# Row gathers of AUGRU steps 4 to 7 moved into the end of the GRU, one PSUM pool per AUGRU bank, and the first AUGRU stages on named banks

## The chip, the cores and the metric

One of the cores of a Trainium2 chip runs the whole program. The metric is the device time of one execution in microseconds (us). The kernel before takes 2083.58 us, the median of 3 runs (2083.48 to 2083.83).

## The reference

A recommender in the manner of DIEN, for 1024 users with histories of 100 items, 128 features each, all in float32:

```python
# keys: a GRU over the history, T = 100 steps, H = 128
r, z = sigmoid(i_r + h_r), sigmoid(i_z + h_z)
n = tanh(i_n + r * h_n)
h = (1 - z) * n + z * h
# attention: a 512 -> 80 -> 40 -> 1 MLP on [keys, q, keys - q, q * keys], masked softmax over t
pooled = einsum('bt,btd->bd', attn, keys)
att_seq = pooled.T[:T]            # step t's weights are feature t of pooled
# AUGRU over the keys, with step t's weight a_t for each user
r, u = sigmoid([h, x_t] @ Wr.T + br), sigmoid([h, x_t] @ Wu.T + bu)
h_hat = tanh([h * r, x_t] @ Wh.T + bh)
u = a_t * u
h = (1 - u) * h + u * h_hat
# the state at each user's last item goes with user, item and history sums into a
# 640 -> 200 -> 80 -> 1 MLP of sigmoids
```

The weights of the AUGRU's first step are a feature of the finished pooled sum. So the AUGRU's recurrence cannot begin before the softmax over all 100 steps is done.

## The kernel before, in words

**Layout.** Features lie on the 128 partitions, users along the free dimension, in two halves of 512 columns (`HB`, `NH` = 2). A half is one matmul's width and one PSUM bank. Weights and states are float32, for which a matmul appears as two passes in the trace. The order of instructions on each engine is the order in which the program text issues them (`manual_schedule`); pools of tiles say which memory is reused when, and waits follow from that.

**GRU phase** (`gru_phase`). 100 steps, each for both halves: gate matmuls (L490), activations on ACT (L502 to L522), sums on DVE. Around a step lie the attention MLP of earlier steps, the history sums on POOL (L476, L477) and the pooling. Each step's state is transposed in blocks of 32 (`Half.transpose`, L529) into a buffer of four steps, `kt`, pool `kp`, and stored in DRAM as `keys_d`: the first two groups of four steps (q = 0 and 1, which are steps 0 to 3 and 4 to 7) as rows of 512 floats per user, later ones in blocks. The softmax runs over blocks of steps that end at `ENDS`; `Half.pool` multiplies a buffered key by its weight `e` (L586) and adds it to `pooled` (L587), on POOL, and in the tail of the phase (after the loop) on POOL for half 0 and DVE for half 1. The last lines multiply by the lengths' mask into `s_b` (L919) and prepare the stores to `pooled_d`; half 1's four are issued on SP (L923).

**Sorting.** The AUGRU works on users sorted by length, so that late steps are narrower. Rows of `keys_d` and of `pooled_d` come in sorted order by indirect DMAs on POOL (`gather`, L135): 128 rows of 512 floats (256 KB) for a key row gather `rows`, four for each half and q (`load_rows`, L146). The rows of q = 0 are gathered two a step from step 70 (`GATHER`) on; those of q = 1 by `all_of(gathers(1))` in the AUGRU phase.

**AUGRU phase** (`augru_phase`, L925). It begins with the hand-over, in this order of text: `load_key(0, i)` transposes step 0's keys on TensorE (L1006, tile `pk`) and copies them on ACT (L1007); half 0's four stores to `pooled_d` on ACT's queue (L1167); eight gathers of `att_r` from `pooled_d` on POOL; `first_step` (L947, L949), matmuls and activations of step 0, which has no state yet; step 1's keys; `open_gates` (L1020), the input parts of step 1's gates; `first_state` (L962 to L974), which spreads step 0's weights over the partitions by matmuls (`first`, `spare`) and makes the first state h; then the eight row gathers of q = 1. The loop calls `half_step` (L1036) for each step and half: the state's part of the gates (L1024), the reset product, the next half's `open_gates`, loads of the weights of step t + 2, and `load_key(t + 1, i)`. In step 1 `store_weights` also turns `att_r` over (tile `pw` or `spare`, L984), copies it (`att_t`, L986) and stores it for the later loads.

Seven PSUM banks come from one pool `ps3` in turn, an eighth from `pa3`. The GRU phase's tail had six banks from its pool `ps` (`last`) and two from `pa`. SBUF buffers of the AUGRU's keys come from `qp3` (four buffers).

Of the kernel before, what the change touches and what calls it, by code (L numbers as in the profile page):

```python
# [9 lines left out]
F32 = mybir.dt.float32  # L10
# [15 lines left out]
GH = HB // P  # L26

R = 32
KH = HB // R
NK = B // R  # L30
A0, A1 = 80, 40
M0, M1 = 200, 80
# [19 lines left out]
G = 4  # L52
# [3 lines left out]
FIRST = [sum(READ[:q]) for q in range(len(READ))]  # L56
# [9 lines left out]
ALIVE = [[min(HB, 2 * -(-r // (2 * EIGHTH))) for r in room] for room in ROOM] + [[HB] * T]  # L66
WIDTHS = [[max(LEAST, n) for n in alive] for alive in ALIVE]

PR = P // NH


@with_exitstack
def kernel(ctx: ExitStack, tc: tile.TileContext, a: dict, out: bass.AP):
# [26 lines left out]
    nc = tc.nc  # L100
# [21 lines left out]
    ident = const.tile([P, P], F32, name="ident")  # L122
# [5 lines left out]
    idx_p = const.tile([P, HB // PR], I32, name="idx_p")  # L128
    h3 = [const.tile([P, HB], F32, name=f"h3_{i}") for i in range(NH)]
    mid = ctx.enter_context(tc.tile_pool(name="mid", bufs=2))  # L130
    later = {}

    def gather(dst, src, g, i):
# [8 lines left out]
    rows = {}  # L142

    def load_rows(q, i, width, tiles):

        n = READ[q]  # L146
        if q < WHOLE:
            tag = "whole" if q else "once"
            r = rows[q, i] = tiles.tile([P, GH, n * P], F32, tag=tag, name="rows", bufs=NH)
            for g in range(GH):  # L150
                gather(r[:, g, :], keys_d[q], g, i)
                yield
            return
# [12 lines left out]

    def all_of(steps):
        for _ in steps:
            pass

    def gru_phase(pools):
# [31 lines left out]
        hp = pools.enter_context(tc.tile_pool(name="hp", bufs=6))  # L203
        wp = pools.enter_context(tc.tile_pool(name="wp", bufs=2))
        sp = pools.enter_context(tc.tile_pool(name="sp", bufs=2))
        kp = pools.enter_context(tc.tile_pool(name="kp", bufs=8))
        ps = pools.enter_context(tc.tile_pool(name="ps", bufs=6, space=PSUM))
        pa = pools.enter_context(tc.tile_pool(name="pa", bufs=2, space=PSUM))

# [233 lines left out]
        class Half:  # L443
# [85 lines left out]
            def transpose(self, t):  # L529


                q, n = divmod(t, G)
                h = self.h.pop(t) if t < T - 1 else self.h[t]
                if n == 0:
                    self.kt[q] = kp.tile([P, KH, G, R], F32, name="kt")
                kt = self.kt[q]
                nc.vector.transpose(kt[:, :, n, :], h.rearrange("p (k r) -> p k r", r=R))
                if q < WHOLE:
                    to = keys_d[q][self.cols, :].rearrange(
                        "(k r) (n a c) -> n a r k c", r=R, n=G, c=R  # L540
                    )
# [97 lines left out]
        banks = {}  # L639
# [153 lines left out]

        rest = load_later()
        early = [load_rows(0, i, HB, mid) for i in range(NH)]

        late, again, early_from = 6, 24, 84
        for s in range(T):
            last = s == T - 1
            n, due = divmod(s - again, 4)  # L800
            n, i = divmod(n, NH)
# [46 lines left out]
            for half in halves:  # L848
                if last:
                    half.cross_features()  # L850
            for half in halves:
                half.pool(2 if len(half.todo) > 7 or s >= 92 else 1, nc.gpsimd)
                if s >= GATHER:
                    next(early[half.i], None)
# [9 lines left out]
        def some(*these):  # L864
            for f in these:
                next(features[f])

        take(T - 2)
        for half in halves:
            half.product(T - 1)  # L870
# [12 lines left out]
        n = ENDS[-3] - ENDS[-4] + 1  # L883
# [33 lines left out]
        for half in reversed(halves):  # L917
            t = blocked(s_bs[NH * (soft["j"] % 2) + half.i])
            nc.vector.tensor_mul(t, later["used"][:, half.ks, :], pooled[:, half.ks, :])  # L919
            to = pooled_d[half.cols, :].rearrange("(k r) (p c) -> p r k c", r=R, c=R)  # L920
            later["att", half.i] = [(to[p], t[p * R : (p + 1) * R]) for p in range(P // R)]
        for to, t in later["att", 1]:
            nc.sync.dma_start(out=to, in_=t)  # L923

    def augru_phase(pools, widths, alive):  # L925


        wp = pools.enter_context(tc.tile_pool(name="wp3", bufs=3))
        qp = pools.enter_context(tc.tile_pool(name="qp3", bufs=4))
        sp = pools.enter_context(tc.tile_pool(name="sp3", bufs=2))  # L930
        kp = pools.enter_context(tc.tile_pool(name="kp3", bufs=4))
        ps = pools.enter_context(tc.tile_pool(name="ps3", bufs=7, space=PSUM))
        pa = pools.enter_context(tc.tile_pool(name="pa3", bufs=1, space=PSUM))
        wr, wu, wh = later["wr"], later["wu"], later["wh"]
        keys, att, opened, resets, states = {}, {}, {}, {}, {}
        later["pace"] = None

        def bank(name):
            return ps.tile([P, HB], F32, tag="g", name=name)

        def first_step(i):

            k = keys.pop((0, i))
            gates = []
            for n, f in (("u", AF.Sigmoid), ("h", AF.Tanh)):
                p = bank(f"p{n}")
                nc.tensor.matmul(p, lhsT=later["w" + n][:, 1, :], rhs=k, start=True, stop=True)  # L947
# [47 lines left out]
            )  # L995
            att[t, i] = at

        def load_key(t, i):

            q = max(j for j, first in enumerate(FIRST) if first <= t)  # L1000
            w, n, r = widths[t], t - FIRST[q], rows[q, i]
            k = qp.tile([P, HB], F32, name="k3")
            if q < WHOLE:
                p = pa.tile([P, HB], F32, tag="a", name="pk3")
                for g in range(-(-w // P)):
                    nc.tensor.transpose(p[:, ts(g, P)], r[:, g, ts(n, P)], ident)  # L1006
                nc.scalar.copy(k[:, :w], p[:, :w])  # L1007
            else:
                w = -(-w // R)
                nc.vector.transpose(  # L1010
                    k.rearrange("p (k r) -> p k r", r=R)[:, :w, :], r[:, :w, ts(n, R)]
                )
            keys[t, i] = k

        def open_gates(t, i):

            k = keys.pop((t, i))[:, : widths[t]]
            for m, name in ((wr, "pr"), (wh, "ph"), (wu, "pu")):
                p = opened[t, i, name] = bank(name)[:, : widths[t]]
# [15 lines left out]
        def half_step(t, i):  # L1035


            w, h = widths[t], h3[i][:, : widths[t]]
# [30 lines left out]
                store_weights(1, spare)  # L1069
            if t + 2 < T:  # L1070
                load_att(t + 2, i)
            if t + 1 < T:
                load_key(t + 1, i)

        def last_state(i):
# [4 lines left out]
        def predict(g, last=False):  # L1080
# [1 line left out]

            m0, m1 = later["m0"], later["m1"]
            n = M0 // MC
            pool, tag = (ps, "g") if last else (pa, "a")

            def rows_of(out_ap, in_ap, o, i):
                nc.gpsimd.indirect_dma_start(  # L1088
# [10 lines left out]
            p0 = [pool.tile([P, HB], F32, tag=tag, name="p0") for _ in range(n if last else 1)]  # L1099
# [34 lines left out]
            p1 = pool.tile([P, HB], F32, tag=tag, name="p1")[:M1, :P]  # L1134
# [8 lines left out]
            p2 = pool.tile([P, HB], F32, tag=tag, name="p2")[:, 0:1]  # L1143
# [18 lines left out]


        for i in range(NH):
            load_key(0, i)
        for to, t in later["att", 0]:
            nc.scalar.dma_start(out=to, in_=t)  # L1167
# [12 lines left out]
        for t in range(1, T):  # L1180
# [109 lines left out]
```

## Time and profile before

| | |
|---|---|
| median of 3 runs | 2083.58 us |
| profiled execution | 2087.38 us, of which its span 2085.5 us |
| mean granted TensorE clock | 0.993 |
| DVE, ACT, POOL busy | 84%, 40%, 63% of the span |
| DMA | 205.09 MB, mean 98 GB/s |
| a GRU step in mid-phase | 14.07 us |

The profile is one execution. Its page gives each engine's busy time as a share of the span, and the span in 40 slices with a digit for the busy tenths. Groups of instructions by line follow, with the mean time of one and the idle time before it. A timeline lists single instructions: start, length, engine, line, operation, output and inputs, and in brackets the idle time of the engine before it and what ended that. A name such as `ACTq` or `SPq` is the stretch in which an engine issues DMAs; "PEld" is the weight load that goes with a matmul; "remote" and "issue" are idle time that the profile puts down to no instruction of another engine. Ends of matmuls are modelled from their issue.

Some costly groups near the change:

| line, engine | what | number | mean |
|---|---|---|---|
| L586 POOL | key times weight | 191 | 1148 ns |
| L587 POOL | add to pooled | 191 | 1332 ns |
| L490 PE | gate matmul, input part | 1200 | 603 ns |
| L135 POOL | indirect gather, `rows` at 1465 us | 8 | 950 ns, with 300 ns between two |

### The profile page before, as it was taken

What the parts mean: (1) busy time and instruction counts of PE and PEld (TensorE: products, weight loads), DVE (VectorE), ACT (ScalarE), POOL (GpSimd) and SP (SyncE); (2) the same over time, 40 slices, a digit from 0 to 9 for tenths busy, and PEclk for the clock granted to TensorE, in tenths of its full rate; (3) what the DMA queues carried; (4) which work ended last, traced back from release to release, by engine and by line L of the source; (5) the groups of instructions that cost most, each with busy time, mean ns of one, the idle gap of its engine ahead of it and who ended that gap; (6) DMA issues with size and microseconds to landing.
All of it is one profiled execution on the core that took longest, in us unless ns stands there. A gap on an engine that the chain in (4) does not pass through costs nothing. (4 is left out here: it accounts for less than half of the span.)

```text
span 2085.5 us, 26811 instructions
## 1 busy us (share of the span) xinstructions
PE 2039.8 (98%) x8320; PEld 980.6 (47%) x8320; DVE 1755.5 (84%) x3050; ACT 831.7 (40%) x1516; POOL 1304.6 (63%) x1306
## 2 busy tenths in 40 slices
PE   8999999999999999999999999997899999999997
PEld 3343333333333333333333333333444556678897
DVE  6888999989989888989889899997467777888786
ACT  3334343333434333433333343333343444445454
POOL 0234939579796959595969687986635444444332
PEclk9999999999999999999999999998999999999999
DMA  4633233332234334333433222332533333334331
GB/s 119 114 93 100 90 102 110 95 98 84 89 106 112 109 103 121 110 95 110 132 98 102 82 81 89 102 93 72 150 95 110 97 93 96 98 98 97 78 73 35
DMA packets 254324, 205.09 MB, mean 98 GB/s; under 512 B 75814, under 2 KB 216842, under 8 KB 254170
## 3 DMA queue, kind: packets, MB, share of 16 engines
q1 hardware_dynamic: 239738, 170.57, 29.2%
q0 software_dynamic: 12320, 32.44, 5.6%
q8 instruction: 68, 1.11, 0.2%
q14 instruction: 86, 0.70, 0.1%
q10 hardware_dynamic: 2112, 0.26, 0.1%
HBM read 147.16 MB, written 54.40 MB: 97 GB/s over the span
## 5 line engine op out<-in xcount | busy, mean ns | idle before, releaser
L490 PE MATMUL ps<-x,wih 128*128 128x512 f32 x1200 | 592.6, 603 | 4.0 <-DMA x<-in_hist_x 4.0
L490 PE MATMUL ps<-hn,whh 128*128 128x512 f32 x1188 | 574.4, 592 | 0.0
L490 PEld LDWEIGHTS ps<-x,wih 128*128 128x128 f32 x1200 | 220.9, 191 | 327.5 <-issue 253.0
L490 PEld LDWEIGHTS ps<-hn,whh 128*128 128x128 f32 x1188 | 225.7, 190 | 284.1 <-issue 275.8
L476 POOL TENSOR_TENSOR xm<-x,m 128x512 f32<-128x512 f32 x200 | 247.2, 1236 | 136.3 <-DMA m<-mask_d 136.0
L521 ACT ACTIVATE ps<-ps,bih 128x512 f32<-128x512 f32 x200 | 132.4, 662 | 486.6 <-DVE ps L520 486.6
L502 ACT ACTIVATE r<-ps,brz 128x512 f32<-128x512 f32 x200 | 137.5, 687 | 372.9 <-PE ps L490 372.1
L477 POOL TENSOR_TENSOR hist<-hist,xm 128x512 f32<-128x512 f32 x200 | 266.7, 1333 | 15.7
L587 POOL TENSOR_TENSOR pooled<-pooled,kw 128x512 f32<-128x512 f32 x191 | 254.4, 1332 | 15.0
L586 POOL TENSOR_TENSOR kw<-kt,e 128x512 f32<-128x512 f32 x191 | 219.3, 1148 | 70.3 <-DVE e L759 70.2
L159 POOL DMA_INDIRECT rows<-keys_d,idx_k x208 | 202.3, 973 | 83.8 <-POOL rows L158 53.0
L563 DVE TENSOR_TENSOR kq<-hn,item 128x512 f32<-128x512 f32 x200 | 228.5, 1182 | 0.0
L650 PE MATMUL pm<-hn,wk 128*32 128x512 f32 x1200 | 212.0, 596 | 3.5 <-ACT q L233 1.8
L650 PE MATMUL pm<-kq,wkq 128*32 128x512 f32 x1200 | 209.6, 592 | 0.0
L1032 ACT ACTIVATE c<-ph,bh 128x96 f32<-128x96 f32 (+42 forms) x198 | 96.9, 489 | 262.2 <-PE ph L1024 227.7
L650 PE MATMUL pm<-mv,w 128*32 128x512 f32 (+1 forms) x808 | 196.5, 598 | 1.4 <-DVE e L740 1.4
L158 POOL COPY rows<-rest 128x1 f32<-128x1 f32 x208 | 39.1, 188 | 222.1 <-DVE rest L1061 218.1
L1048 DVE TENSOR_TENSOR pu<-pu,c 128x96 f32<-128x96 f32 (+42 forms) x197 | 88.8, 451 | 103.6 <-ACT c L1032 85.0
L684 DVE TENSOR_TENSOR f<-pm,q 128x512 f32<-128x512 f32 x200 | 128.3, 683 | 51.2 <-PE pm L650 51.1
L525 DVE TENSOR_TENSOR d<-hn,ps 128x512 f32<-128x512 f32 x198 | 135.9, 687 | 34.8 <-ACT ps L521 32.5
L526 DVE TENSOR_TENSOR d<-ps,d 128x512 f32<-128x512 f32 x200 | 138.4, 692 | 23.6 <-ACT ps L522 6.4
L520 DVE TENSOR_TENSOR ps<-ps,u 128x512 f32<-128x512 f32 x200 | 140.0, 700 | 21.6 <-PE ps L490 0.5
(180 smaller groups left out, 3028.3 us busy)
## 6 DMA issues: line engine op xcount, KB each, us to landing
x<-in_hist_x SPq DMA_DIRECT2D x212, 256.0 KB
keys_d<-kt SPq DMA_DIRECT2D x46, 1024.0 KB
m<-mask_d SPq DMA_DIRECT2D x200, 128.0 KB
keys_d<-kt SPq DMA_DIRECT2D x64, 64.0 KB
rows<-keys_d,idx_k POOLq DMA_INDIRECT x208
s_b<-mv SPq DMA_DIRECT2D x200, 8.0 KB
mask_i<-in_mask SPq DMA_DIRECT2D x8, 200.0 KB
at<-att_d SPq DMA_DIRECT2D x32, 48.0 KB
```

The source lines that it names most:

```text
L159: nc.gpsimd.indirect_dma_start(out=r[:, k, :], out_offset=None, in_=keys_d[q], in_offset=bass.IndirectOffsetOnAxis(ap=idx_k[:, k, i : i + ...
L476: nc.gpsimd.tensor_mul(d, x, m)
L477: nc.gpsimd.tensor_add(acc, acc, d)
L490: nc.tensor.matmul(p, lhsT=w[:, g, :], rhs=v, start=(j == 0), stop=(j == len(parts) - 1),)
L502: nc.scalar.activation(r, pr, AF.Sigmoid, bias=brz[:, 0:1])
L520: nc.vector.tensor_add(pi, pi, u)
L525: nc.vector.tensor_sub(d, h, pi)
L526: nc.vector.tensor_mul(d, pz, d)
L563: nc.vector.tensor_mul(kq, h, item[:, self.cols])
L586: eng.tensor_mul(d, k, w)
L587: eng.tensor_add(acc, acc, d)
L650: nc.tensor.matmul(p[i][s, :], lhsT=w[:, s], rhs=v, start=start, stop=stop)
```

## The change

The rows of q = 1 are gathered in the GRU phase: four gathers (half 0) in step 98 (`T - 2`) ahead of that step's pooling, four (half 1) after the loop. Their buffers are two `kt` buffers in a pool of its own, `kx`, which also serves the key groups with q % 4 == 1; `kp` shrinks from eight buffers to six. Each AUGRU bank becomes a pool with one buffer; a ring hands them out, and the first stages name their banks. `first_step` and step 1's key copies now stand ahead of half 0's pooled stores on ACT, of which one goes to SP. `open_gates(1, 1)` stands ahead of `open_gates(1, 0)`. Step 2's keys are transposed before `first_state` and no longer in step 1. The pool of AUGRU keys grows from four to six buffers. `predict` takes its banks by a helper, with the same tiles as before.

```diff
+EARLY_BANKS, LATE_BANKS = (2, 5, 6, 0), (3, 4, 1)
...
+    kx = ctx.enter_context(tc.tile_pool(name="kx", bufs=NH))
...
-            tag = "whole" if q else "once"
-            r = rows[q, i] = tiles.tile([P, GH, n * P], F32, tag=tag, name="rows", bufs=NH)
+            tag = "kt" if q else "once"
+            r = rows[q, i] = tiles.tile([P, GH, n * P], F32, tag=tag, name="rows")
...
-        kp = pools.enter_context(tc.tile_pool(name="kp", bufs=8))
+        kp = pools.enter_context(tc.tile_pool(name="kp", bufs=3 * NH))
...
-                    self.kt[q] = kp.tile([P, KH, G, R], F32, name="kt")
+                    self.kt[q] = (kx if q % 4 == 1 else kp).tile(
+                        [P, KH, G, R], F32, tag="kt", name="kt"
+                    )
...
         early = [load_rows(0, i, HB, mid) for i in range(NH)]
+        more_early = [load_rows(1, i, HB, kx) for i in range(NH)]
...
+            if s == T - 2:
+                all_of(more_early[0])
             for half in halves:
                 half.pool(2 if len(half.todo) > 7 or s >= 92 else 1, nc.gpsimd)
...
+        all_of(more_early[1])
         take(T - 2)
...
-        for to, t in later["att", 1]:
+        for to, t in later["att", 1] + later["att", 0][G - 1 :]:
             nc.sync.dma_start(out=to, in_=t)
...
-        qp = pools.enter_context(tc.tile_pool(name="qp3", bufs=4))
+        qp = pools.enter_context(tc.tile_pool(name="qp3", bufs=3 * NH))
...
-        ps = pools.enter_context(tc.tile_pool(name="ps3", bufs=7, space=PSUM))
+        ps = [
+            pools.enter_context(tc.tile_pool(name=f"ps3_{n}", bufs=1, space=PSUM))
+            for n in range(7)
+        ]
...
-        def bank(name):
-            return ps.tile([P, HB], F32, tag="g", name=name)
+        ring = [*LATE_BANKS, *EARLY_BANKS]
+
+        def bank(name, n=None):
+
+            if n is None:
+                n = ring.pop(0)
+                ring.append(n)
+            return ps[n].tile([P, HB], F32, tag="g", name=name)
...
-                p = bank(f"p{n}")
+                p = bank(f"p{n}", EARLY_BANKS[NH * i + j])
...
-                p = pa.tile([P, HB], F32, tag="a", name="pk3")
+                p = pa.tile([P, HB], F32, tag="a", name="pk3") if n is None else bank("pk3", n)
...
-            if t + 1 < T:
+            if 1 < t < T - 1:
                 load_key(t + 1, i)
...
         for i in range(NH):
-            load_key(0, i)
-        for to, t in later["att", 0]:
+            load_key(0, i, (None, EARLY_BANKS[NH])[i])
+        gates = [first_step(i) for i in range(NH)]
+        for i in range(NH):
+            load_key(1, i, (EARLY_BANKS[0], None)[i])
+        for to, t in later["att", 0][: G - 1]:
             nc.scalar.dma_start(out=to, in_=t)
         sorted_rows = [gather_weights(i) for i in range(NH)]
-        gates = [first_step(i) for i in range(NH)]
+        open_gates(1, 1, EARLY_BANKS)
+        open_gates(1, 0, LATE_BANKS)
         for i in range(NH):
-            load_key(1, i)
-        for i in range(NH):
-            open_gates(1, i)
-        spare = bank("spare")
+            load_key(2, i)
+        spare = bank("spare", EARLY_BANKS[-1])
         first_state(0, pa.tile([P, HB], F32, tag="a", name="first"))
         first_weights(0, spare)
-        all_of(gathers(1))
         ahead, due = gathers(2), spread(2)
```

More of the change, by code (lines that the diff above doesn't have):

```diff
@@ L944, in first_step @@
             gates = []
-            for n, f in (("u", AF.Sigmoid), ("h", AF.Tanh)):
-                p = bank(f"p{n}")
+            for j, (n, f) in enumerate((("u", AF.Sigmoid), ("h", AF.Tanh))):
+                p = bank(f"p{n}", EARLY_BANKS[NH * i + j])
                 nc.tensor.matmul(p, lhsT=later["w" + n][:, 1, :], rhs=k, start=True, stop=True)
@@ L996, in load_att, with load_key @@
             att[t, i] = at
-        def load_key(t, i):
+        def load_key(t, i, n=None):
             q = max(j for j, first in enumerate(FIRST) if first <= t)
-            w, n, r = widths[t], t - FIRST[q], rows[q, i]
+            w, m, r = widths[t], t - FIRST[q], rows[q, i]
             k = qp.tile([P, HB], F32, name="k3")
             if q < WHOLE:
-                p = pa.tile([P, HB], F32, tag="a", name="pk3")
+                p = pa.tile([P, HB], F32, tag="a", name="pk3") if n is None else bank("pk3", n)
                 for g in range(-(-w // P)):
-                    nc.tensor.transpose(p[:, ts(g, P)], r[:, g, ts(n, P)], ident)
+                    nc.tensor.transpose(p[:, ts(g, P)], r[:, g, ts(m, P)], ident)
                 nc.scalar.copy(k[:, :w], p[:, :w])
@@ L1010, in load_key, with open_gates @@
                 nc.vector.transpose(
-                    k.rearrange("p (k r) -> p k r", r=R)[:, :w, :], r[:, :w, ts(n, R)]
+                    k.rearrange("p (k r) -> p k r", r=R)[:, :w, :], r[:, :w, ts(m, R)]
                 )
             keys[t, i] = k
-        def open_gates(t, i):
+        def open_gates(t, i, banks=(None,) * 3):
             k = keys.pop((t, i))[:, : widths[t]]
-            for m, name in ((wr, "pr"), (wh, "ph"), (wu, "pu")):
-                p = opened[t, i, name] = bank(name)[:, : widths[t]]
+            for m, name, n in zip((wr, wh, wu), ("pr", "ph", "pu"), banks):
+                p = opened[t, i, name] = bank(name, n)[:, : widths[t]]
                 nc.tensor.matmul(p, lhsT=m[:, 1, :], rhs=k, start=True, stop=False)
@@ L1084, in predict, with of_pool @@
             n = M0 // MC
-            pool, tag = (ps, "g") if last else (pa, "a")
+            tag = "last" if last else "a"
+            def of_pool(name):
+                return bank(name) if last else pa.tile([P, HB], F32, tag="a", name=name)
             def rows_of(out_ap, in_ap, o, i):
@@ L1098, in predict @@
             f0 = sp.tile([MC, n, P], F32, name="f0")
-            p0 = [pool.tile([P, HB], F32, tag=tag, name="p0") for _ in range(n if last else 1)]
+            p0 = [of_pool("p0") for _ in range(n if last else 1)]
             p0 = [p0[j if last else 0][:MC, ts(0 if last else j, P)] for j in range(n)]
@@ L1133, in predict @@
             yield
-            p1 = pool.tile([P, HB], F32, tag=tag, name="p1")[:M1, :P]
+            p1 = of_pool("p1")[:M1, :P]
             for j in range(n):
@@ L1142, in predict @@
             yield
-            p2 = pool.tile([P, HB], F32, tag=tag, name="p2")[:, 0:1]
+            p2 = of_pool("p2")[:, 0:1]
             nc.tensor.matmul(p2, lhsT=f1, rhs=later["m2"], start=True, stop=True)
```

## The prediction

> **What bounds the kernel now.** I read the page's busy table and slices first, then the table by stage, the waits and the timeline of the one stretch that the change touches. Lines (L) are those of the kernel before; times are on the profile's axis.
>
> ```profile
> span 2085.5 us, 26811 instructions
> ...
> PE 2039.8 (98%) x8320; PEld 980.6 (47%) x8320; DVE 1755.5 (84%) x3050; ACT 831.7 (40%) x1516; POOL 1304.6 (63%) x1306
> ...
> PE   8999999999999999999999999997899999999997
> ...
> PEclk9999999999999999999999999998999999999999
> ```
>
> TensorE (PE) is busy 98% of the span, so outside a few places an edit on another engine is worth nothing. The slices show one place: slices 28 and 29 (7 and 8 tenths), about 1408 to 1512 us, where the GRU hands over to the AUGRU. The change acts there, or just ahead of it. The table by stage (PE, PE weight loads, DVE, ACT and POOL busy us, granted clock, DMA share, GB/s) gives its inside:
>
> ```profile
> 1440.00:1448.00 8.00, 1.11 (x4) 0.71 (x4) 7.62 (x15) 0.93 (x2) 7.47 (x7) 0.50 0.44 138
> 1448.00:1454.00 6.00, 5.99 (x8) 2.60 (x9) 1.28 (x2) 2.36 (x3) 0.00 (x0) 0.55 0.54 87
> ...
> 1465.00:1470.00 5.00, 2.73 (x15) 1.66 (x13) 0.69 (x1) 1.70 (x3) 3.78 (x5) 1.00 0.62 164
> 1470.00:1478.00 8.00, 2.82 (x6) 1.25 (x6) 1.29 (x2) 0.70 (x3) 3.51 (x4) 0.57 0.69 195
> ```
>
> So PE has two holes. In the first (1440 to 1448) it waits for the pooling, on which DVE and POOL are both full. In the second (1465 to 1478) no engine is full, while the DMA share is 0.62 to 0.69. The timeline of that second stretch (start, length, instruction, and in brackets the idle time and what ended it):
>
> ```profile
> 1448.01 2.07 PE L947 MATMUL pu<-k,wu 128*128 128x512 f32 x2 [6.50 <-DVE pooled L587]
> ...
> 1449.31 2.05 ACTq L1167 DMA_DIRECT2D pooled_d<-s_b  x4
> ...
> 1454.59 0.99 POOL L135 DMA_INDIRECT att_r<-pooled_d,idx  x1 [6.81 <-PE ph L947]
> ...
> 1464.15 1.12 PE L1024 MATMUL pr<-h,wr 128*128 128x512 f32 x2 [0.69 <-DVE h L974]
> 1464.68 0.95 POOL L135 DMA_INDIRECT rows<-keys_d,idx  x1 [0.30 <-issue]
> ...
> 1465.98 0.60 PE L984 MATMUL pw<-ident,att_r 128*128 128x128 f32 x4
> ...
> 1468.14 0.66 ACT L1044 ACTIVATE pr<-pr,br 128x512 f32<-128x512 f32 x1 [1.51 <-PE spare L962]
> ...
> 1473.77 0.69 DVE L986 COPY att_t<-pw 128x512 f32<-128x512 f32 x1 [4.24 <-remote]
> ...
> 1478.13 0.69 DVE L974 TENSOR_TENSOR h<-spare,first_h 128x512 f32<-128x512 f32 x1
> ```
>
> The reader should see consumers that start long after their producer. `pr` ends at 1465.3 and ACT reads it at 1468.14 (2.8 us late); `pw` ends at 1466.6 and DVE reads it at 1473.77 (7.2 us late); the second half's `spare` (1466.68, 1.16 long) is read at 1477.40, over 9 us late. The trace's semaphore events say the same: PE's completions arrive late here, by 2.5 to 9 us, and elsewhere in the run by no more than 0.5 us (1.5 us once, near 1892). The stretch is that of the eight row gathers, 256 KB each, issued 1464.68 to 1474.43. From 1480 on PE is full, so what the second hole loses the whole kernel loses.
>
> **The change, part by part.**
>
> *Eight row gathers leave the hand-over.* Two batches of four move into POOL's program: one ahead of the pooling of step 98, one after the last step. A batch costs 4 × (0.95 + 0.30 issue) = 5.0 us of POOL. Before, POOL idles 5.86 us ahead of the L586 at 1395.94 (it waits for `e`, L759), and 5.80 us ahead of the L576 at 1423.09 (same kind of wait). Both hold a batch, 0.8 us to spare: cost taken 0. Were the cover gone, POOL's pooling would be late by 5 us at most, and the pooled sum ends 1447.8 on POOL and 1448.0 on DVE, both on the path. The gathers' buffers were free before (pooled by 1407), and their rows were stored long ago, so nothing queued behind them waits for a transfer. Whether their DMA makes PE late where PE is full, at 1390 to 1396, is not shown. The nearest row is the row gathers of keys 0, two a step in steps 70 to 73, where a step stays 14.07 us: 0. The far end is the hand-over's own lag, some 9 us for two batches, so 4.5 for this one. A gain I exclude: PE has no wait there that a gather could shorten. I take 0, the row nearest in its surroundings (PE full), and keep +4.5.
>
> *What their going gives.* If the lag goes with them, `spare` is read about 1.2 us after its start instead of 10.7: some 9 us on h of the second half (L974, 1478.13).
>
> Here a rule speaks against the change. The Trainium skill, "SBUF — State Buffer", section "SBUF: two separate sides", says that engine ports and DMA ports are disjoint: a transfer cannot slow a compute instruction, and only the port shared by DVE and GpSimd causes waits. By the rule the row gathers cannot delay PE, the lag stays, and this part is worth 0. By the rows the lag and the row gathers' packets (until 1477.7) share one place in 2085 us. I follow the rows: a completion that comes late need not be a slow port. But the lag begins before the first of these transfers could have moved much, which keeps the rule alive as a rival.
>
> *First AUGRU matmuls on banks named early.* `first_step` (L947) now takes banks 2, 5, 6 and 0. In the built changed program its first matmul still waits for DVE's last pooled sum (1447.96): banks that lay in one pool are released together. Only bank 6 lay in another pool, so the second half's first key transpose no longer waits for the first one's copy; both lie in PE's idle time, gain 0. One wait is new: with six key buffers instead of four, ACT's copy of the first key (1439.76 before) overlaps POOL's pooling scratch and waits for POOL's last pooled sum, 1446.52 + 1.27 = 1447.8. Then the copies end 1448.45 and 1449.0, and `first_step` starts 1448.5 instead of 1448.0: −0.5 us. It takes 6.4 us as before (8 passes at half clock, since PE still idles through 1440 to 1448), until about 1455.
>
> *The pooled rows' stores.* Half 0's four stores on ACT become three on ACT and one on SP. Before, ACT issued them at 1449.31, ahead of `first_step`'s activations. Now they stand behind both `first_step`s and the two copies of step 1's keys. ACT: table load 1.28 (at 1449.05), activations until 1455.6, two copies of 0.59 until 1456.8, three issues of some 0.5 each until 1458.1, landing 2.0 us later as before (1451.36 to 1453.37): 1460. The first `att_r` gather follows 1.0 to 1.2 us later: 1461.0 instead of 1454.59. That is +6.4 us on all eight `att_r` gathers, since POOL waits at the first.
>
> *Key transposes moved up.* Step 2's two (four passes of 0.11 and a copy, each) move ahead of `first`, into PE's wait for `att_r`: the second's 0.43 us leaves the dense part.
>
> *The sum.* Before, the last `att_r` gather ends its issue at 1464.4 and landed 1465.75. Plus 6.4: 1472.2. Then `spare` for half 1, four passes of 0.11 twice, about 1.0: 1473.2; L973 and L974 0.70 + 0.69: h1 at 1474.6, before 1478.8. Half 0 is not later: `first` at 1461.52 + 6.4 = 1467.9, h0 1470.3, its gates and reset about 1473. So h1 gains 4.2 us, with the 0.43 us of transposes 4.6. Against this stands the clock. In the trace PE's quiet stretch 1467.2 to 1470.6 is followed by 0.50 until 1477.4. The Trainium skill, "TensorE: Matmul & The Clock Gate", section "Part 1: The HAM clock gate", has a free-running window of some 3.4 us: one idle window halves the clock, one busy window restores it. After the change PE idles 1464 to 1467.9 and is thin until 1474. By the rule `pr`, `spare` and the first dense passes may run at half clock: −0.9 to −2 us in the worst phase; by a clock at 1.00 throughout 0. I take −0.3, as the thin stretch holds more matmuls than before, and −2 for the range. Gain 4.3 us.
>
> The profiled execution lasted 2087.38 us (span 2085.5, 1.9 around it): 2083.1 after. It stands 3.8 us above the median of the runs, of which I assume it is a plain offset: 2083.58 − 4.3 = 2079.3 us.
>
> **The rivals.**
>
> *The late stores cost nothing* (chance 0.16). ACT's issues fall earlier than I chain them, or `first_step` starts before the pooling ends. For it: the diff names banks that are free early. Against: the waits of the built program, and ACT's order. Then `att_r` lands as before at 1465.8, `spare` is read about 1467.9, h1 at 1469.3: gain 9.5, less up to 2 for the clock: 2074.1 to 2076.
>
> *The change gives back what it takes* (0.12). Four back-to-back gathers make PE late in step 98 by up to 4.5 us, or a part of the lag remains with the `att_r` gathers. Gain 0 to 3: 2080.6 to 2083.6. For it: PE's completions lagged already when the last `att_r` gathers were in flight. Against: the gathers of steps 70 to 73.
>
> *Slower: the lag isn't the row gathers'* (0.08). As the rule has it, the lag belongs to something else that stays, say the first run through the AUGRU's code. Then the +6.4 us of the late stores on ACT's queue stands alone: `spare` at 1472.2 + 1.0 + 9 = 1482.2, h1 1483.6 against 1478.8, +4.8, less 0.4 of transposes, plus the clock's 0 to 1: 2088 to 2089. It decides as soon as more than some 4.5 us of `spare`'s lag remains; for it speaks the lag's early start, against it that the lag ends with the row gathers' packets.
>
> **How the numbers follow.** My forecast has 0.64: gain 3 to 5.5, 2078 to 2080.6. A measurement of this kernel can tell about 0.2%, 4.2 us: 2079.4 and 2087.8. Of the forecast's own chance some 0.42 lies below 2079.4 and 0.22 above. Faster: 0.42 + 0.16 = 0.58. Same: 0.22 + 0.12 = 0.34. Slower: 0.08. The range takes in the first rival (2073.5) and the second with a clock loss of 2 us on top (2085.5), and leaves out the slower case and the tails.
>
> **What would show it.** Right: POOL's two idle gaps at 1390 and 1417 filled by row gathers, with the GRU's end still at 1448; `first_step` still behind DVE's last pooled sum; ACT's three stores at about 1457; the first `att_r` gather near 1461; `pr`, `pw` and `spare` read within 1 us of their ends; h1 near 1475, and PE full a microsecond later. Wrong: an `att_r` gather before 1456 (first rival), the pooling's end past 1449 or a longer step 98 (second), or readers of `pr` and `pw` still several us late with no row gather in flight (third).

## The result and the profile after

The changed kernel takes 2075.61 us, the median of 6 runs (2074.65 to 2076.30), beside 2083.78 us for the kernel before: ratio 0.996, 95% interval 0.9947 to 0.9973, 8.2 us less. The forecast was 4.3 us less, 2079.3, in a range from 2073.5 to 2085.5. The profiled execution took 2075.50 us, its span 2073.7.

The page first: the span, PE's busy tenths by slice, and its granted clock.

```profile
span 2073.7 us, 26805 instructions
...
PE   8999999999999999999999999997999999999998
...
PEclk9999999999999999999999999999999999999999
```

Slice 29 has gone from 8 to 9 tenths; slice 28 still has 7. The table by stage (columns as before: PE, weight loads, DVE, ACT, POOL, clock, DMA share, GB/s) says what is left of the two holes:

```profile
1440.00:1448.00 8.00, 0.00 (x0) 0.00 (x0) 7.29 (x17) 0.48 (x2) 7.69 (x8) 0.66 0.59 183
1448.00:1454.00 6.00, 4.32 (x7) 2.02 (x8) 2.45 (x4) 3.73 (x5) 1.01 (x1) 0.60 0.32 55
...
1465.00:1470.00 5.00, 3.76 (x20) 2.37 (x20) 1.39 (x2) 1.10 (x2) 3.52 (x4) 1.00 0.20 56
1470.00:1478.00 8.00, 7.33 (x33) 4.30 (x32) 7.26 (x11) 3.41 (x6) 2.52 (x5) 1.00 0.40 114
```

The first hole (1440 to 1448) is still there, and now wholly empty (0.00 of 8 us, 1.11 before). The second is closed: from 1470 to 1478 PE is busy 7.33 of 8 us instead of 2.82, at a granted clock of 1.00 instead of 0.57.

The timeline of POOL in step 98, before (first line) and after, shows the moved gathers:

```profile
1395.94 1.07 POOL L586 TENSOR_TENSOR kw<-kt,e 128x512 f32<-128x512 f32 x1 [5.86 <-DVE e L759]
...
1390.57 0.99 POOL L140 DMA_INDIRECT rows<-keys_d,idx  x1
...
1394.83 0.96 POOL L140 DMA_INDIRECT rows<-keys_d,idx  x1 [0.30 <-issue]
...
1395.81 1.09 POOL L583 TENSOR_TENSOR pooled<-pooled,e 128x512 f32<-128x512 f32 x1
```

Four of them fill what was POOL's wait, and the pooling goes on 0.02 us after the last. Against the profile before, DVE's instructions stand 1.25 us later from 30 us on, 1.38 us just before the gathers and 1.23 us at the GRU's end. That offset is older than the gathers, so they cost nothing. The timeline of the hand-over:

```profile
1448.50 0.69 DVE L594 TENSOR_TENSOR pooled<-pooled,last 128x512 f32<-128x512 f32 x1
...
1449.68 2.07 PE L969 MATMUL pu<-k,wu 128*128 128x512 f32 x2 [10.47 <-ACT k L1029]
...
1455.87 0.35 ACTq L1196 DMA_DIRECT2D pooled_d<-s_b  x1
1455.98 0.60 ACT L1029 COPY k<-pk 128x512 f32<-128x512 f32 x1
1456.26 1.05 ACTq L1196 DMA_DIRECT2D pooled_d<-s_b  x2
...
1459.65 0.99 POOL L140 DMA_INDIRECT att_r<-pooled_d,idx  x1 [10.63 <-DMA pooled_d<-s_b]
...
1464.50 0.93 PE L984 MATMUL first<-ident,att_r 128*128 128x128 f32 x6 [0.68 <-issue]
...
1468.49 0.95 POOL L140 DMA_INDIRECT att_r<-pooled_d,idx  x1 [0.30 <-issue]
...
1469.87 0.60 PE L1006 MATMUL pw<-ident,att_r 128*128 128x128 f32 x4
...
1470.95 0.69 DVE L1008 COPY att_t<-pw 128x512 f32<-128x512 f32 x1
```

`pw` ends at 1470.47 and DVE reads it at 1470.95. Before, it read 7.2 us after the end.

To compare executions whose GRU ends at different times, I count from the end of DVE's last pooled sum (1449.19 here, 1447.95 before). All rows are from the traces, in us. The first two columns are the starts of the first `att_r` gather and of the matmuls `first`. The columns h0 and h1 are the starts of the multiplications that finish the halves' first states. "step 51" is the start of the DVE instruction that makes half 1's state of AUGRU step 51 (`h`, L1074; L1052 before), and "to the end" is from there to DVE's last drain, at the program's end.

| kernel | first att_r | first | h0 | h1 | step 51 | to the end |
|---|---|---|---|---|---|---|
| before | +6.64 | +13.56 | +15.46 | +30.18 | +438.13 | 198.9 |
| after | +10.46 | +15.31 | +18.12 | +23.09 | +430.60 | 193.4 |
| row gathers early alone | +6.24 | +13.58 | +15.47 | +20.64 | +428.59 | 194.5 |
| after, row gathers back | +10.94 | +15.47 | +18.72 | +32.79 | +442.50 | 194.1 |
| after, stores first | +6.37 | +16.25 | +18.49 | +23.32 | +430.83 | 194.0 |
| after, one bank pool | +10.98 | +15.82 | +18.71 | +24.06 | +431.57 | 194.2 |
| row gathers early, keys early | +6.31 | +10.84 | +14.06 | +19.47 | +427.48 | 193.9 |
| the same, stores split | +6.37 | +10.45 | +14.15 | +19.39 | +427.39 | 193.1 |
| row gathers early, 8 gathers of 64 KB | +6.24 | +13.57 | +15.47 | +29.59 | +438.46 | 193.5 |
| row gathers early, 4 gathers of 64 KB | +6.33 | +13.56 | +15.45 | +24.80 | +434.25 | 194.8 |
| row gathers early, 4 plain loads | +6.32 | +13.57 | +15.46 | +20.79 | +428.80 | 193.6 |
| before, paced row gathers | +6.67 | +13.56 | +15.46 | +26.06 | +437.95 | 201.2 |
| row gathers early, all in step 98 | +6.31 | +13.62 | +15.52 | +20.91 | +428.87 | 199.8 |
| row gathers early, 8 of 64 KB behind step 1 | +6.31 | +13.56 | +15.46 | +20.29 | +428.25 | 189.1 |

The hand-over gives 30.18 − 23.09 = 7.1 us at h1, and 0.4 us more in step 1, where two key transposes are gone: 7.5 us by step 51. From step 2 to step 51 the distances between all fourteen traces stay the same to 0.1 us, so step 51 carries what a hand-over is worth. From step 52 on the traces part, by up to 12 us, also where no edit reaches. There TensorE's completions, the semaphore events by which it reports an instruction's end, come late again, by 0.5 to 1.6 us at most, in every trace but the one of the fourth chip. So of the 8.2 us, 7.5 are accounted for by the hand-over, and less than 1 is not separated from that spread.

### The profile page after: what moved, and what is told of

The parts are those of the page before. It is cut to its first block, busy times and chain, and to the rows that moved or that the text cites. A ratio compares the mean times of both kernels' runs of the same rounds, so it can differ in the third digit from the quotient of the medians.

```text
span 2073.7 us, 26805 instructions
## 1 busy us (share of the span) xinstructions
PE 2037.9 (98%) x8320; PEld 980.9 (47%) x8320; DVE 1757.8 (85%) x3050; ACT 831.7 (40%) x1516; POOL 1306.9 (63%) x1306
## 3 DMA queue, kind: packets, MB, share of 16 engines
q8 instruction: 68, 1.11, 0.2%
```

## The experiments

Theory A: POOL's row gathers, standing where they did, make TensorE's completions late, and the change gains by taking them away, while its new order of stores gives part of it back. Theory B, from the rule on separate ports: the lag is something else's, and the gain comes from the new order. The kernels of one group ran on one chip, with the kernel before beside them (the changed kernel itself was not measured again there); the four chips differ (the kernel before took 2083.3, 2084.2, 2089.8 and 2067.4 us), so times are compared within a group and by ratio.

### First group (before: 2083.31 us)

**The row gathers alone.** The kernel before with what the change does to `kx`, `kp`, `load_rows`, step 98 and the loop's end, and nothing else:

```diff
...
+            if s == T - 2:
+                all_of(more_early[0])
...
+        all_of(more_early[1])
         take(T - 2)
...
         first_weights(0, spare)
-        all_of(gathers(1))
```

> The kernel before with one part of the change alone: the eight row gathers in step 98 and after the loop, with the buffers that go with it. Theory A (the row gathers make TensorE's completions late at the hand-over): the lag goes, att_r still starts at about 1454.6 us, spare is read near 1468 instead of 1477, gain 8 to 9.5 us, 2074 to 2076 us, as much as the whole change or more. Theory B (the lag belongs to something that stays, and the gain came from the new order): within 1.5 us of 2083.7.

Measured: 2072.81 us, ratio 0.9948 (0.9934 to 0.9961), 10.5 us less than before. This one part alone is worth at least as much as the whole change (0.996, intervals overlapping); by the hand-over it is 2.5 us better at h1 (+20.64 against +23.09) and 2.0 us by step 51. Its timeline:

```profile
1447.02 0.69 DVE L590 TENSOR_TENSOR pooled<-pooled,last 128x512 f32<-128x512 f32 x1
...
1453.95 0.99 POOL L136 DMA_INDIRECT att_r<-pooled_d,idx  x1 [6.42 <-PE pk L1013]
...
1461.29 1.05 PE L969 MATMUL first<-ident,att_r 128*128 128x128 f32 x8
...
1465.75 0.60 PE L991 MATMUL pw<-ident,att_r 128*128 128x128 f32 x4
...
1467.02 0.68 DVE L993 COPY att_t<-pw 128x512 f32<-128x512 f32 x1
1467.62 0.69 DVE L980 TENSOR_TENSOR spare<-spare,first_u 128x512 f32<-128x512 f32 x1
...
1468.35 0.69 DVE L981 TENSOR_TENSOR h<-spare,first_h 128x512 f32<-128x512 f32 x1
```

`first` stands at +13.6 as before, and `pw` and `spare` are read about 0.7 us and 0.4 us after their ends. h1 is 9.5 us earlier than before, and so is step 51. Theory B has fallen.

**The row gathers back.** The changed kernel with its eight row gathers behind `att_r` again:

```diff
-        more_early = [load_rows(1, i, HB, kx) for i in range(NH)]
+        later["more"] = [load_rows(1, i, HB, kx) for i in range(NH)]
...
-            if s == T - 2:
-                all_of(more_early[0])
...
-        all_of(more_early[1])
...
         first_weights(0, spare)
+        for steps in later["more"]:
+            all_of(steps)
```

> The changed kernel with the row gathers back behind the att_r gathers, all else as changed. Theory A: the lag returns, a few us of it cut off because TensorE's first step is nearly over when they start: 2080 to 2085 us. Theory B: 2075.6 within 1 us, and pr, pw and spare read within 1 us of their ends.

Measured: 2088.14 us, ratio 1.0024 (1.0015 to 1.0033): slower than the kernel before, outside what I had expected of theory A by 3 us. The lag returned whole (h1 9.7 us later than in the changed kernel, step 51 11.9 us later), and none of it was cut off as I had thought. The buffers stayed as changed, so it isn't they that took the lag away:

```profile
1468.08 0.96 POOL L140 DMA_INDIRECT rows<-keys_d,idx  x1 [0.30 <-issue]
...
1469.48 1.06 PE L981 MATMUL spare<-ident,att_r 128*128 128x128 f32 x8
1469.94 0.69 DVE L1005 COPY att_t<-pw 128x512 f32<-128x512 f32 x1 [0.18 <-issue]
...
1476.89 0.96 POOL L140 DMA_INDIRECT rows<-keys_d,idx  x1 [0.31 <-issue]
1479.08 0.70 DVE L992 TENSOR_TENSOR spare<-spare,first_u 128x512 f32<-128x512 f32 x1 [8.44 <-remote]
...
1479.81 0.69 DVE L993 TENSOR_TENSOR h<-spare,first_h 128x512 f32<-128x512 f32 x1
```

`pw`, which ends at 1469.6 during the second row gather, is read 0.3 us later. `spare` of half 1, done by its modelled end at 1470.5, is read at 1479.08, 1.2 us after the issue of the last gather. The trace's semaphore events agree: PE's completions arrive at 1472.8, 1476.3, 1479.1 and 1479.8, one after another. (Some events are missing from a trace. In the kernel before, five of them come together, from 1477.3 to 1477.5.) The last event of the attention rows that `spare` reads is at 1469.9, so it isn't waiting for data.

**The stores first.** The changed kernel with ACT's three stores ahead of `first_step`:

```diff
+        for to, t in later["att", 0][: G - 1]:
+            nc.scalar.dma_start(out=to, in_=t)
         gates = [first_step(i) for i in range(NH)]
```

> The changed kernel with ACT's three stores of the pooled rows put back ahead of first_step's activations. If they are on the path, the first att_r gather starts some 4 us earlier (near 1455.6 instead of 1459.7 in the changed kernel's profile) and the time falls by 3 to 4 us, to 2071.5 to 2072.5. If another wait (first_step, the open gates) is last anyway, within 1 us of 2075.6.

Measured: 2074.59 us, ratio 0.9957 (0.9943 to 0.9970), no clear difference from the changed kernel's 0.996. The timeline of this kernel says why:

```profile
1455.37 0.99 POOL L140 DMA_INDIRECT att_r<-pooled_d,idx  x1 [6.56 <-PE pu L969]
...
1457.39 1.12 PE L1042 MATMUL pr<-k,wr 128*128 128x512 f32 x2 [0.86 <-ACT k L1029]
...
1464.20 0.95 POOL L140 DMA_INDIRECT att_r<-pooled_d,idx  x1 [0.30 <-issue]
...
1465.25 1.16 PE L984 MATMUL first<-ident,att_r 128*128 128x128 f32 x8 [0.68 <-issue]
```

`att_r` now starts 4.1 us earlier after the pooled sum, and the last gather is issued before `first` even begins. `first` stands behind TensorE's own program: six open gates from 1457.39 on, then step 2's key transposes with a copy between them. In the row gathers alone `first` comes at +13.58, here at +16.25, and step 2's transposes and copies fill the 2.6 us before it. That they are the cause is read from the trace: no run puts them alone back behind `first`. Where the stores go late, this program is nearly as late, so neither alone is the bound.

**One pool of banks.** The changed kernel with one pool `ps3` of seven banks, handed out in turn:

```diff
+        ps = pools.enter_context(tc.tile_pool(name="ps3", bufs=7, space=PSUM))
...
-            return ps[n].tile([P, HB], F32, tag="g", name=name)
+            return ps.tile([P, HB], F32, tag="g", name=name)
```

> The changed kernel with the seven AUGRU banks in one pool again, handed out in turn. If the named banks bring nothing, as I read the built program (first_step waits for the last pooled sum either way): 2075.6 within 0.7 us. If they let a stage start earlier: slower by 1 us or more.

Measured: 2076.71 us, ratio 0.9966 (0.9952 to 0.9979), 1.1 us above the changed kernel, with intervals that overlap. In the trace the second key transpose now waits for the pooled sum, which ends at 1446.75, and `first_step` stands behind it:

```profile
1447.00 1.09 PE L1022 MATMUL pk<-ident,rows 128*128 128x128 f32 x4 [10.66 <-DVE pooled L594]
...
1447.88 1.92 PE L963 MATMUL pu<-k,wu 128*128 128x512 f32 x2
```

`first_step` starts at +1.13 instead of +0.49, and h1 and step 51 come 1.0 us later. So by the trace the named banks bring 1 us, through bank 6, which lets the transpose go ahead and `first_step` start 0.6 us earlier; the times don't settle it.

### Second group (before: 2084.16 us)

**Keys of step 1 early.** To the row gathers alone I added one move:

```diff
         for i in range(NH):
             load_key(0, i)
+        for i in range(NH):
+            load_key(1, i)
         for to, t in later["att", 0]:
...
         gates = [first_step(i) for i in range(NH)]
-        for i in range(NH):
-            load_key(1, i)
```

> The kernel before with the row gathers early, and step 1's key transposes and copies moved ahead of the pooled stores, into the time in which TensorE waits for the pooling. In the profile of the row gathers alone, the open gates start at 1456.1 because of these copies and first at 1461.3, while the half's att_r had landed by about 1460. If TensorE's program is what is last there: first near 1460.1, 1 to 1.4 us less, 2071.4 to 2071.8 us. If the att_r gathers are last for the second half anyway: within 0.5 us of 2072.8.

Measured: 2071.04 us, ratio 0.9936 (0.9922 to 0.9949). h1 comes at +19.47, 1.2 us earlier, as expected of TensorE's program being last:

```profile
1459.81 1.11 PE L969 MATMUL first<-ident,att_r 128*128 128x128 f32 x6
...
1465.59 0.60 PE L991 MATMUL pw<-ident,att_r 128*128 128x128 f32 x4
...
1466.64 0.69 DVE L993 COPY att_t<-pw 128x512 f32<-128x512 f32 x1 [0.32 <-PE spare L969]
...
1468.44 0.69 DVE L981 TENSOR_TENSOR h<-spare,first_h 128x512 f32<-128x512 f32 x1
```

`first` is issued at +10.84 instead of +13.58 and now waits for the att_r rows as they land. This version is 13.1 us below the kernel before on its chip. Against the changed kernel it is 3.1 us ahead by step 51; by ratio it is ahead too (0.9936 against 0.996), but the intervals still touch.

**One store split off as well.**

```diff
-        for to, t in later["att", 1]:
+        for to, t in later["att", 1] + later["att", 0][G - 1 :]:
...
-        for to, t in later["att", 0]:
+        for to, t in later["att", 0][: G - 1]:
```

> The kernel just described with one of half 0's four pooled stores moved from ACT's queue to SP's, as in the change. ACT's last issue ends some 0.5 us earlier, and the att_r gathers start with it: 0.4 us less, 2071.0 to 2071.4 us; if SP's fifth store lands last instead, no difference. Against both kernels: 12 us below the kernel before, 4 below the changed one.

Measured: 2071.69 us, ratio 0.9939 (0.9926 to 0.9953): no difference. The first `att_r` gather starts at +6.37 with five stores on SP and at +6.31 with four.

**Gathers of a quarter of the size.** The row gathers alone, and in their old place eight that nobody reads:

```diff
+        for i in range(NH):
+            r = kp.tile([P, GH, P], F32, tag="none", name="none", bufs=NH)
+            for g in range(GH):
+                gather(r[:, g, :], pooled_d, g, i)
```

> The kernel before with the row gathers early, and in their old place eight gathers that nobody reads, of 64 KB each (from the pooled rows) instead of 256 KB. If the lag of TensorE's completions goes with the bytes: a quarter of it or none, 2073 to 2075.5 us. If it goes with the number of gathers that POOL issues: all of it, 2081 to 2084 us.

Measured: 2083.18 us, ratio 0.9995 (0.9987 to 1.0003): the whole loss is back with a quarter of the bytes.

```profile
1465.11 0.95 POOL L136 DMA_INDIRECT none<-pooled_d,idx  x1 [0.30 <-issue]
...
1466.82 0.60 PE L991 MATMUL pw<-ident,att_r 128*128 128x128 f32 x4
...
1473.89 0.95 POOL L136 DMA_INDIRECT none<-pooled_d,idx  x1 [0.30 <-issue]
1475.41 0.69 DVE L993 COPY att_t<-pw 128x512 f32<-128x512 f32 x1 [5.60 <-remote]
...
1478.38 0.69 DVE L981 TENSOR_TENSOR h<-spare,first_h 128x512 f32<-128x512 f32 x1
```

`pw` ends at 1467.4 and is read at 1475.41, 0.6 us after the last of the eight. By step 51 the eight cost 9.9 us.

**Plain loads.** The row gathers alone, and four loads of 256 KB on SP in that place, held until h0 by a copy that each overwrites:

```diff
+        r = kp.tile([P, GH, G * P], F32, tag="none", name="none", bufs=1)
+        for g in range(GH):
+            nc.vector.tensor_copy(r[:, g, 0:1], h3[0][:, 0:1])
+        for g in range(GH):
+            nc.sync.dma_start(out=r[:, g, :], in_=keys_d[1][ts(g, P), :])
```

> The kernel before with the row gathers early, and in their old place four plain loads of 256 KB on SP's queue that nobody reads, begun when the first half's state is ready. If any transfer of that size makes TensorE's completions late there: half of the lag, 2076 to 2079 us. If only POOL's gathers do: within 1.5 us of 2072.8.

Measured: 2073.28 us, ratio 0.9948 (0.9934 to 0.9961), the same as the row gathers alone.

```profile
1464.04 3.34 SPq L1188 DMA_DIRECT2D none<-keys_d  x4
...
1465.59 0.60 PE L991 MATMUL pw<-ident,att_r 128*128 128x128 f32 x4
...
1467.03 0.68 DVE L993 COPY att_t<-pw 128x512 f32<-128x512 f32 x1
...
1468.36 0.69 DVE L981 TENSOR_TENSOR h<-spare,first_h 128x512 f32<-128x512 f32 x1
```

With four loads in flight `pw` is read 0.8 us after its end. From 1463.5 to 1470 the loads' queue moved 1.15 MB in 626 packets; the queue of the gathers of 64 KB moved 0.60 MB in 302 packets in twice the time (1464.5 to 1478), and there the loss was whole. So it is neither bytes nor packets as such, but the indirect gathers that POOL issues. Whether it is their being indirect or their coming from POOL is not separated: no run issues plain loads from POOL.

### Third group (before: 2089.77 us)

**Paced.** The kernel before, with a copy of one column ahead of each row gather:

```diff
+                if q:
+                    nc.gpsimd.tensor_copy(r[:, g, 0:1], ident[:, 0:1])
                 gather(r[:, g, :], keys_d[q], g, i)
```

> The kernel before, with a copy of one column (128x1) on POOL ahead of each of the eight row gathers, which stay in their old place. Later row gathers of the AUGRU, one copy ahead of each, run at a pitch of 1.45 us and TensorE's completions do not lag beside them; these run at 1.26. If the lag needs gathers back to back: it goes, 2073 to 2076 us. If any gather of POOL makes it there: 2083 to 2086 us.

Measured: 2089.94 us, ratio 1.0001 (0.9994 to 1.0008): no help. In its profile h1 is 4.1 us earlier than in the profile before, but readers are late in step 1 behind it, and by step 51 it stands where the kernel before does (+437.95 against +438.13). So gathers with a copy between them make the same lag here.

**Four gathers instead of eight.** As the gathers of a quarter of the size, but one half's only (`gather(r[:, g, :], pooled_d, g, 1)`).

> The kernel before with the row gathers early, and in their old place four gathers of 64 KB that nobody reads, instead of eight. If each further gather costs its share: half of the 10.4 us that eight cost, 2077 to 2079 us. If the lag holds until POOL's burst ends: 5 us less than with eight, the same. If it needs a burst longer than 12: 2073 us; if the first few do it: 2082 us.

Measured: 2079.81 us, ratio 0.9951 (0.9938 to 0.9965), 10.0 us less than before: by the time, four gathers cost nothing. The trace has the lag:

```profile
1474.08 0.69 DVE L981 TENSOR_TENSOR h<-spare,first_h 128x512 f32<-128x512 f32 x1
```

This is h1, at +24.80: 4.2 us more than with none (+20.64), where eight cost 9.0 (+29.59). By step 51 four cost 5.4 us against the next kernel, on the same chip, and eight 9.9 us: 1.2 to 1.4 us a gather, near POOL's pitch of 1.26. In the other experiments of the first three groups the gain in time over the kernel before and the gain at step 51 over its profile agree within 2.5 us; here they are 6 us apart. So what a single gather costs rests on this trace and is not confirmed by the times.

**All eight in step 98.**

```diff
-                all_of(more_early[0])
+                for steps in more_early:
+                    all_of(steps)
...
-        all_of(more_early[1])
```

> The kernel before with the row gathers early, but all eight back to back in step 98 of the GRU, where TensorE is full. POOL's idle time there, 5.9 us, holds four; the pooling behind is some 4.5 us late and may catch up in its second idle time: 2073 to 2078 us. If a long burst of gathers makes completions late wherever it stands, TensorE loses another 5 us or more in step 98: 2078 to 2084 us.

Measured: 2080.14 us, ratio 0.9954 (0.9940 to 0.9970), with h1 at +20.91. Its POOL timeline:

```profile
1388.00 0.99 POOL L136 DMA_INDIRECT rows<-keys_d,idx  x1
...
1397.30 0.96 POOL L136 DMA_INDIRECT rows<-keys_d,idx  x1 [0.30 <-issue]
...
1398.27 1.09 POOL L579 TENSOR_TENSOR pooled<-pooled,e 128x512 f32<-128x512 f32 x1
```

The burst runs 10 us beside a full TensorE, and DVE, which reads TensorE's results, keeps its place: from 1388 to 1396 it stands 1.2 to 1.4 us ahead of the profile before, as ahead of the burst. The time, on a chip 6 us slower, does not decide between the two bands; the ratio and the trace speak against a lag. But the pooling behind the burst stands about 5 us behind the profile before, and this is not wholly caught up: from 1421 on DVE stands 0.3 us behind that profile, so the GRU's end loses 1.5 us, which the two batches of the change do not.

So a burst of eight makes no lag in the GRU. That alone does not put the lag down to the hand-over's surroundings. There, too, the eight `att_r` gathers by themselves make completions at most 0.7 us late (in the changed kernel); the loss came with 12 and 16 gathers in a row. Whether the length of the burst or the work beside it decides stays open: no run puts more than eight in a row into the GRU.

### Fourth chip (before: 2067.36 us)

**Eight gathers behind step 1.** The quarter-size gathers again, but after `half_step(1, 1)`.

> The kernel before with the row gathers early, and eight gathers of 64 KB that nobody reads behind step 1 of the AUGRU, where TensorE is full with 512-column matmuls again, instead of in the hand-over. If a burst of gathers makes TensorE's completions late anywhere in the AUGRU: some 9 us, as in the hand-over, and readers several us late between 1472 and 1485. If it needs the hand-over's thin work: within 1.5 us of the row gathers alone (ratio to the kernel before 0.9948).

Measured: 2068.45 us, ratio 1.0002 (0.9994 to 1.0011), by the expectation a loss as in the hand-over. The trace speaks against that reading:

```profile
1467.02 0.60 PE L991 MATMUL pw<-ident,att_r 128*128 128x128 f32 x4
...
1467.66 0.69 DVE L993 COPY att_t<-pw 128x512 f32<-128x512 f32 x1
...
1469.29 0.69 DVE L981 TENSOR_TENSOR h<-spare,first_h 128x512 f32<-128x512 f32 x1
```

Up to the AUGRU's end no completion in this trace comes later than 0.25 us after a modelled end, neither beside the eight gathers nor beside the `att_r` gathers, nor in the steps from 52 on, and step 51 stands where the row gathers alone have it (+428.25 against +428.59). It is the kernel before that is fast here: 16 to 22 us below its times on the other chips. It seems that this chip doesn't have the lag, so the run doesn't tell where a burst hurts. That the change would gain nothing there is likely, but neither the changed kernel nor a trace of the kernel before was taken on it.

## Why the prediction was right, point by point

**The moved gathers cost nothing:** shown, by DVE's place, which is no later behind the gathers than ahead of them (1.38 us, then 1.23 us behind the profile before). The GRU's end at 1449.19 lies past the 1449 that I had named as a sign of the second rival, but only by that older offset. All eight in step 98 cost the GRU 1.5 us in their run, so the split into two batches matters.

**The lag goes with the row gathers:** shown both ways, by taking them alone away (9.5 us earlier by step 51) and by putting them back (11.9 us later). The rule of the Trainium skill ("SBUF — State Buffer", section "SBUF: two separate sides") that no transfer slows a compute instruction made 0 of this part. It holds for the plain loads (h1 within 0.15 us) and would have misled for gathers issued by POOL. Following the rows was right, but their reading as a matter of DMA traffic was not: I had pointed to the DMA share and to packets in flight, and neither bytes nor packets decide. My reading that completions elsewhere are at most 0.5 us late, but for once near 1892, was too tidy: in the profile before they are also 1.1 us late near 1932 and 0.8 near 1960.

**Banks and the new wait:** `first_step` still starts behind the last pooled sum. It starts at +0.49 instead of +0.06: the 0.5 us that I had put down for ACT's copies. Bank 6, for which I had taken 0, is worth 0.6 us at `first_step` once that wait is there.

**The pooled rows' stores:** here lies the step that failed, in its size and in its path. I had the first `att_r` gather 6.4 us later; counted from the pooled sum it came 3.8 us later. The missing 2.6 us are: `first_step` took 5.2 us (1449.68 to 1454.89) instead of 6.4, as full clock returned after its first half (its last two matmuls take 1.02 us each, the first 2.07); ACT's issues began at 1455.87, beside the second key copy (1455.98) and not behind it; and the first gather came 2.3 us after the last issue instead of 2.9. The first two put the last issue at +8.1 instead of +10.2. And I had all of this delay on the path to h1. It is not: with the stores first, `att_r` starts 4.1 us earlier, and h1 and step 51 come no earlier (0.2 us later). The new order does give back 2.0 us by step 51 against the row gathers alone, but it gives back as much without the late stores: TensorE's own program is longer, with step 2's transposes before `first`, where I had booked them as a gain in idle time.

**The key transposes** that left step 1 gave 0.4 us, as forecast (0.43).

**The clock** cost nothing: 1.00 throughout from 1454 on. TensorE's thin stretch before `first` did not lower it, so the 0.3 us that I took off was too much.

**Sum:** the hand-over gave 7.5 us by step 51 instead of the 4.3 forecast: 2.6 by the smaller delay of the stores, 0.3 by the clock, and 0.3 that no single term has. So the sign and the main term were right and the give-back was too large. The time, 2075.6, is in the range, but outside my own forecast's band (2078 to 2080.6). It lies in the first rival's band (2074.1 to 2076), and there by luck: that rival's mechanism was an `att_r` gather before 1456, and the stores did go late.

**The slower rival** (the lag stays) needed theory B and is excluded on the chips where the lag shows. Late stores with the lag kept gave 1.0024, 4.8 us above the kernel before, as its sum had it; by the trace it is 2.6 us at h1 and 4.4 by step 51, so its number came out, while its delay of 6.4 us did not.

What stays open is why POOL's gathers make TensorE's completions late here and not in the GRU, and why one chip shows none of it. As the ends of matmuls are modelled, the traces do not tell either whether the matmuls themselves ran late or only the news of their end.

## What to carry to other kernels

Where a reader starts microseconds after its producer's modelled end while no engine is full, ask what is being issued in that time, and move that, before rearranging the order around it. Try the parts of a change singly: here one part was worth 9.5 us in the hand-over and the rest gave 2.0 of it back. Compare where the traces run in step again, here from step 2 to step 51, and set the times beside it. A gain that rests on such a lag should be measured on more than one chip.

## What the runs showed of the hardware

TensorE's completions came up to more than 9 us late while POOL issued indirect gathers in the hand-over. By step 51 the loss was 9.5 us for eight of 256 KB, 9.9 for eight of 64 KB, 5.4 for four of 64 KB (by one trace, which the times do not confirm), and 0.2 for four plain loads of 256 KB from SP. Eight gathers in a row beside 512-column matmuls of the GRU made no such lag, and the eight `att_r` gathers of the hand-over by themselves made at most 0.7 us of it.

The same kernel took 2067.4, 2083.3, 2084.2 and 2089.8 us on four chips. On the fastest one no lag of this kind was in the trace of its variant.
